# A two-layer graph kernel on one core: layer 0's attention logits laid out with neighbours on partitions

## The chip, the cores and the metric

The kernel runs on one core of a Trainium2 chip. The metric is the device time of one execution in microseconds (us), the median of a few runs of the whole kernel. TensorE (PE) does the matrix products, VectorE (DVE) and ScalarE (ACT) the element-wise work and the reading of PSUM, GpSimd (POOL) some element-wise work on SBUF, and SyncE (SP) issues all DMAs. Each of these runs its own instructions strictly in the order in which the program wrote them.

## The reference, cut to what matters

There are 128 graphs of 64 nodes with 768 features each. Layer 0 is an attention with 12 heads of 64 features, whose logit is a sum of one term of the row node and one term of the neighbour; layer 1 is an ordinary attention with 6 heads.

```python
h = jnp.einsum('bnd,ade->bane', feat_in, W)               # layer 0
th = jnp.tanh(h)
attn = th @ w_src + swapaxes(th @ w_dst, 2, 3)            # [b, a, n, m]: src[n] + dst[m]
attn = jnp.where(attn >= 0, attn, 0.2 * attn)
attn = jnp.where(~adj[:, None], -999.0, attn)
attn = jax.nn.softmax(attn, axis=-1)
feat_out = elu(attn @ h + b)
gate = sigmoid(feat_in @ H_w.T + H_b)
x = layernorm(x + gate * feat_out + (1 - gate) * feat_in)
# layer 1: q, k, v projections, masked softmax attention, output projection,
# residual, layernorm
```

## The kernel before

All arithmetic is float32. The 8192 rows (graph, node) are cut into 64 tiles of 128 rows, so a tile holds two graphs g = 0, 1 of 64 nodes, and two tiles make a pair; there are 32 pairs. Layer 0 runs over the pairs in a software pipeline, then layer 1 runs over groups of four tiles. What passes between the layers (`x1d`, `x1Td`, `vd`) goes through DRAM.

**The order of layer 0.** Each large product (h, the gate g, and layer 1's value v) is a Strassen-like job of seven block products; each of them is three matmuls of 128x384, which the profile shows as six records. The list `TURN` gives the order in which 21 block products are issued in one iteration of the pair loop: h and g of the new pair, v and its rest u of older pairs. Positions 0 to 20 are the places in this list. After each product the earlier one's way out of PSUM is emitted (`flush`, L203), and then the actions that the table `plan` has for this position. So every engine's queue is fixed by this table. In iteration p the new pair's tiles are n0 and n1, and the pair before has t0 and t1; the odd tile goes first.

**What happens to one tile in layer 0.**
- `products` (L354) and `terms` (L363): tanh of h on ACT (L358), two multiplications (L359 on DVE, L360 on POOL), and a reduction (L367) to `sd`, [128, 24]: for each row and head the neighbour ("dst") term and the source ("src") term. The dst terms go to DRAM (`dstd`, L369) and come back broadcast to all 64 rows of their graph (`dd`, [128, 768], two DMAs at L372). SP waits for the first before it issues the second.
- `with_bias` (L380): the bias plus one is added to h on POOL (L383), and half of the heads are copied by two DMAs into `hx` with the graphs exchanged between the partition halves.
- `logits` (L392): one DVE addition makes `att`, rows on partitions, (head, neighbour) along the free dimension. `leaky` (L404) is a Prelu on ACT. `masked` (L408) has three DVE instructions of 768 elements: the predicated copy of -999 (L412), the row maximum (L418), its subtraction (L419). `exps` (L421) is the exponential into `prob`.
- `probs_by_nodes` (L439): six TensorE transposes per tile (helper `transposed`, L432, records at L436), two PSUM banks, two ACT copies (L437) into `pT`, neighbours on partitions.
- `attend` (L450): 24 small matmuls of 64x64 weights by 64x66, in the four quadrants of the array, into two banks `av`; the two extra columns of h are ones and give the softmax's denominator.
- `features`, `elu1`, `gated`, `stats`, `normed`: division (L473, L474), exp (L481), elu (L492), gate and residual (L497, L499), layer norm (L216 to L226). `gate_tanh` (L534) makes the gate on ACT (L537, L538), `residual` (L484) multiplies gate and x on POOL (L487).
- `by_features` (L512): x1 is transposed by six TensorE transposes (`x1Tp`) and two ACT copies for the product v.

`x_sums` (L556) makes the next pair's operand sums on POOL, `value_sums` (L553) those of v on DVE, both through `block_sums` (L143 to L146).

The buffers that matter: the PSUM tag "m" has two banks and is shared by `pTp`, `av` and `x1Tp`; tag "work" has five SBUF buffers of [128, 768].

Of the kernel before, what the change touches and what calls it, by code (L numbers as in the profile page):

```python
# [9 lines left out]
F32 = mybir.dt.float32  # L10
U8 = mybir.dt.uint8
AF = mybir.ActivationFunctionType
ALU = mybir.AluOpType
AX = mybir.AxisListType

P = 128
N = 64
D = 768
KC = D // P
HK = KC // 2  # L20
HALF = D // 2
# [4 lines left out]
J1 = H1 // 2  # L26
LEAKY = 0.2
EPS = 1e-5
NEG0 = -999.0
NEG1 = 9000000000000000.0  # L30
PAIR = 2
GT = 4
# [26 lines left out]
def kernel(  # L59
# [2 lines left out]
    x: bass.AP,  # L62
    xT: bass.AP,
    adj: bass.AP,
    w0: bass.AP,
    b0: bass.AP,
    wsrc: bass.AP,
# [31 lines left out]
    x1_d = [dram.tile([P, PAIR, D], F32, name=f"x1d_{p}") for p in range(NP)]  # L99
    x1T_d = [dram.tile([P, KC, PAIR * P], F32, name=f"x1Td_{p}") for p in range(NP)]  # L100
    v_d = [dram.tile([P, D], F32, name=f"vd_{t}") for t in range(2 * NP)]
    dst_d = [dram.tile([P, H0], F32, name=f"dstd_{t}") for t in range(2 * NP)]


    ident = const.tile([P, P], F32, name="ident")
# [4 lines left out]
    V.memset(minus_one, -1.0)  # L110
    one = const.tile([P, 1], F32, name="one")
    V.memset(one, 1.0)
    neg0 = const.tile([P, 1], F32, name="neg0")
    V.memset(neg0, NEG0)

    def load_cols(src, name):
        t = const.tile([P, KC], F32, name=name)
# [118 lines left out]
    with ExitStack() as ph:  # L236
# [41 lines left out]
        weight_sums(V, wv_w)  # L278

        def work(name):  # L280
            return sb.tile([P, D], F32, tag="work", name=name, bufs=5)

        st = [dict() for _ in range(2 * NP)]

# [78 lines left out]
        def terms(t):  # L363

            th = st[t].pop("th")
            sd = small.tile([P, 2 * H0], F32, tag="sd", name=f"sd_{t}")
            V.tensor_reduce(sd, th.rearrange("p s (a e) -> p (s a) e", e=E0), AX.X, ALU.add)  # L367
            st[t]["sd"] = sd
            nc.sync.dma_start(out=dst_d[t], in_=sd[:, :H0])  # L369
            dd = work(f"dd_{t}")  # L370
            for g in range(2):
                nc.sync.dma_start(  # L372
                    out=dd[g * N : (g + 1) * N, :],
                    in_=dst_d[t][g * N : (g + 1) * N, :]
                    .rearrange("m a -> (m a)")
                    .partition_broadcast(N),
                )
            st[t]["dd"] = dd

        def with_bias(t):  # L380

            h = st[t]["h"]
            G.tensor_tensor(  # L383
                h[:, :, :E0], h[:, :, :E0], b01_bc.unsqueeze(1).to_broadcast([P, H0, E0]), ALU.add
            )

            hx = sb.tile([P, J0, EP], F32, tag="hx", name=f"hx_{t}")
            nc.sync.dma_start(out=hx[:N], in_=h[N:, :J0, :])
            nc.sync.dma_start(out=hx[N:], in_=h[:N, J0:, :])
            st[t]["hx"] = hx  # L390

        def logits(t):  # L392
            sd, dd = st[t].pop("sd"), st[t].pop("dd")
            att = work(f"att_{t}")
            att3 = att.rearrange("p (a m) -> p a m", m=N)
            V.tensor_tensor(
                att3,
                dd.rearrange("p (m a) -> p a m", a=H0),
                sd[:, H0:].unsqueeze(2).to_broadcast([P, H0, N]),
                ALU.add,  # L400
            )
            st[t]["att"] = att

        def leaky(t):  # L404
            att = st[t]["att"]
            S.activation(att, att, AF.Prelu, alpha=LEAKY)

        def masked(t):  # L408

            att = st[t]["att"]  # L410
            att3 = att.rearrange("p (a m) -> p a m", m=N)
            V.copy_predicated(  # L412
                att3,
                st[t]["nadj"].unsqueeze(1).to_broadcast([P, H0, N]),
                neg0.unsqueeze(1).to_broadcast([P, H0, N]),
            )
            mx = small.tile([P, H0], F32, tag="mx", name=f"mx_{t}")
            V.tensor_reduce(mx, att3, AX.X, ALU.max)  # L418
            V.tensor_tensor(att3, att3, mx.unsqueeze(2).to_broadcast([P, H0, N]), ALU.subtract)  # L419

        def exps(t):  # L421

            att = st[t].pop("att")
            prob = work(f"prob_{t}")
            S.activation(
                prob.rearrange("p (j a m) -> p a j m", a=2, m=N),
                att.rearrange("p (a j m) -> p a j m", a=2, m=N),
                AF.Exp,
            )
            st[t]["prob"] = prob  # L430

        def transposed(dst, src, name):  # L432

# [2 lines left out]
                T.transpose(b[:, c * P : (c + 1) * P], src[:, c * P : (c + 1) * P], ident)  # L436
            S.copy(dst, b[:, : 3 * P].rearrange("p (c t) -> p c t", c=3))  # L437

        def probs_by_nodes(t):  # L439
            prob = st[t].pop("prob")  # L440
            pT = sb.tile([P, J0, P], F32, tag="pT", name=f"pT_{t}", bufs=1)
            for half in range(2):
                transposed(
                    pT[:, 3 * half : 3 * half + 3, :],
                    prob[:, half * HALF : (half + 1) * HALF],
                    f"pTp_{t}_{half}",
                )
            st[t]["pT"] = pT

        def attend(t):  # L450
            pT, h, hx = st[t].pop("pT"), st[t].pop("h"), st[t].pop("hx")
            av = [bank("m", f"av_{t}_{a}") for a in range(2)]
            for j in range(J0):
                for a in range(2):
                    rows = slice(a * N, (a + 1) * N)
                    for g in range(2):
                        T.matmul(
                            av[a][g * N : (g + 1) * N, j * EP : (j + 1) * EP],
                            pT[rows, j, g * N : (g + 1) * N],
                            h[rows, a * J0 + j, :] if a == g else hx[rows, j, :],  # L460
                            start=True,
                            stop=True,
                        )
            st[t]["av"] = av
# [60 lines left out]
            nc.sync.dma_start(out=x1T_d[p], in_=x1Ts[p])  # L525

        def mask(p):
            ad = load_adj(sb, 2 * p, PAIR, f"adj_{p}")
            na = sb.tile([P, PAIR, N], U8, tag="nadj", name=f"nadj_{p}", bufs=2)
            V.tensor_scalar(na, ad, 0, None, ALU.is_equal)  # L530
            for i in range(PAIR):
                st[2 * p + i]["nadj"] = na[:, i, :]

        def gate_tanh(t):  # L534

# [27 lines left out]
        for p in range(NP + 2):  # L563
            q = p - 1
            new, old = p < NP, 0 <= q < NP
            t0, t1, n0, n1 = 2 * q, 2 * q + 1, 2 * p, 2 * p + 1
            if new:
                jobs["h"], jobs["g"] = h_job(p), gate_job(p)

            plan = {}  # L570

            def at(pos, ok, *acts):
                if ok:
                    plan.setdefault(pos, []).extend(acts)

            def do(f, *args):
                return lambda: f(*args)

            def v_begins():
                value_sums(q)  # L580
                jobs["v"] = v_job(q)


            at(0, old, do(probs_by_nodes, t1), do(exps, t0), do(gate_tanh, t1))
            at(1, old, do(residual, t1))
            at(2, old, do(attend, t1), do(gate_tanh, t0))
            at(3, old, do(features, t1), do(probs_by_nodes, t0), do(residual, t0))
            at(4, old, do(elu1, t1), do(gated, t1))
            at(5, old, do(attend, t0), do(stats, t1))
            at(6, old, do(features, t0), do(normed, t1))  # L590
            at(7, old, do(elu1, t0), do(gated, t0))
            at(8, old, do(by_features, t1), do(stats, t0))
            at(9, old, do(normed, t0))
            at(12, old, do(v_begins))
            at(15, old, lambda: v_sums[q][0](), lambda: v_sums[q][1](), do(spill_features, q))
            at(16, old, lambda: v_sums[q][2]())
            at(19, old, lambda: v_sums[q][3]())

            at(0, p + 1 < NP, lambda: xTs.__setitem__(p + 1, load_xT(p + 1)))
            at(3, new, do(mask, p))  # L600
            at(4, 0 <= p - 2 < NP, do(spill_values, p - 2))
            at(8, new, do(inputs, p))
            at(11, new, do(products, n1))
            at(11, old, do(by_features, t0))
            at(12, new, do(products, n0))
            at(13, new, do(terms, n1), do(with_bias, n1))
            at(14, new, do(terms, n0), do(with_bias, n0))
            at(15, new, do(plus_one, p))
            at(16, new, do(logits, n1))
            at(17, new, do(leaky, n1))  # L610
            at(17, p + 1 < NP, do(x_sums, p + 1))
            at(18, new, do(masked, n1), do(logits, n0))
            at(19, new, do(exps, n1), do(leaky, n0))
            at(20, new, do(masked, n0))

            for pos, (job, i) in enumerate(TURN):
                ok = {"h": new, "g": new, "v": old, "u": 0 <= p - 2 < NP}[job]
                if ok:
                    step(jobs["u" if job == "u" else job], int(i))
                else:  # L620
                    flush()
                for act in plan.get(pos, ()):
                    act()
            if old:
                jobs["u"] = jobs["v"]
# [290 lines left out]
```

## Time and profile before

| | |
|---|---|
| median of 3 runs | 3061.95 us (3059.85 to 3063.27) |
| the profiled execution | 3063.06 us, of which the span from first to last instruction is 3061.3 us |
| busy in the span | PE 2970.2 us (97%), DVE 1831.3 (60%), ACT 1006.4 (33%), POOL 805.3 (26%) |
| layer 0 | to about 1515 us; one iteration of the pair loop takes 45.6 us |
| one iteration (700 to 746 us) | PE 46.0 of 46.0 us, DVE 38.3, ACT 20.1, POOL 16.5 |
| granted TensorE clock | 0.987 on average, full speed between 100 and 1450 us |

A PE that is shown busy is not proof of a PE at its limit, because matmuls are pipelined and their ends are modelled. The starts of successive groups of matmuls in the timeline are the better measure. The time of the execution is the span and about 1.8 us around it.

### The profile page before, as it was taken

How to read it: one execution, taken by the hardware profiler on the slowest of the kernel's cores; microseconds unless marked ns; L12 is line 12 of the kernel's file. 1: busy time of each engine (PE TensorE's matmuls, PEld its weight loads, DVE VectorE, ACT ScalarE, POOL GpSimd, SP SyncE). 2: the span in 40 equal slices, each digit the busy share in tenths (PEclk: the TensorE clock that was granted, in tenths of full speed). 3: DMA queues.
4: the chain of work that ended last, by engine and by line, in shares of the span. 5: the costliest groups of instructions: out<-in, count | busy, mean ns of one | idle time of the engine just before them, and what ended most of it. 6: DMA issues, size and time to landing. Idle time of an engine off the chain costs nothing. (4 is left out here: it accounts for less than half of the span.)

```text
span 3061.3 us, 42249 instructions
## 1 busy us (share of the span) xinstructions
PE 2970.2 (97%) x16512; PEld 2067.1 (68%) x16512; DVE 1831.3 (60%) x3017; ACT 1006.4 (33%) x1761; POOL 805.3 (26%) x650
## 2 busy tenths in 40 slices
PE   6999999999999999999689999999999999999997
PEld 3666666666666666666378777788777788777784
DVE  5888888888888888888443434343344343344334
ACT  2444444444444444444212222222222222222221
POOL 4333333333333333342112121121212121212111
PEclk8999999999999999999899999999999999999998
DMA  4333333333333333333332211122221222111211
GB/s 166 118 106 115 124 100 115 125 99 115 125 100 117 122 107 117 116 107 111 108 121 69 78 61 56 56 84 83 68 70 45 69 84 78 65 59 51 82 63 62
DMA packets 174917, 284.61 MB, mean 93 GB/s; under 512 B 46208, under 2 KB 112768, under 8 KB 174720
## 3 DMA queue, kind: packets, MB, share of 16 engines
q1 hardware_dynamic: 174720, 281.92, 28.6%
q8 instruction: 131, 2.15, 0.3%
q14 instruction: 66, 0.54, 0.1%
HBM read 167.81 MB, written 101.06 MB: 88 GB/s over the span
## 5 line engine op out<-in xcount | busy, mean ns | idle before, releaser
L487 POOL TENSOR_TENSOR x<-gate,x 128x768 f32<-128x768 f32 x64 | 116.5, 1821 | 331.2 <-ACT gate L538 331.2
L776 POOL TENSOR_TENSOR y<-y,bf_bc 128x768 f32<-128x768 f32 x64 | 114.2, 1815 | 302.7 <-DMA y<-x1d 302.7
L800 DVE TENSOR_TENSOR y<-y_o,y 128x384 f32<-128x384 f32 x128 | 69.8, 554 | 191.1 <-PE y_o L173 183.9
L675 DVE TENSOR_TENSOR kT<-z_k,kT 128x256 f32<-128x256 f32 x96 | 40.6, 423 | 217.3 <-PE z_k L173 109.8
L222 POOL TENSOR_TENSOR rs_b<-ve_b,minus_half 128x1 f32<-128x1 f32 x64 | 35.1, 549 | 498.2 <-DVE ve_b L220 495.3
L173 PE MATMUL y_q<-a,wq 128*128 128x256 f32 x576 | 141.9, 383 | 17.8 <-DMA a<-x1Td 17.8
L143 POOL TENSOR_TENSOR sq_q<-a,a 128x768 f32<-128x768 f32 x16 | 29.5, 1846 | 491.4 <-PE y_o L173 330.5
L360 POOL TENSOR_TENSOR th<-th,wsd 128x768 f32<-128x768 f32 x64 | 115.9, 1812 | 157.8 <-DVE th L359 157.8
L674 ACT ACTIVATE qT<-y_q,bq_c 128x256 f32<-128x256 f32 x144 | 67.3, 468 | 243.6 <-PE y_q L173 221.4
L173 PE MATMUL y_g<-hw,sx_x 128*128 128x384 f32 x384 | 136.2, 492 | 10.5 <-DVE gate L336 10.5
L173 PE MATMUL y_k<-sq_q,wk 128*128 128x256 f32 x576 | 142.8, 385 | 3.7 <-DVE wk L131 3.7
L173 PE MATMUL y_k<-a,wk 128*128 128x256 f32 x576 | 143.5, 385 | 1.8 <-DMA wk<-in_wk_dram 1.8
L173 PE MATMUL y_o<-wf,so_o 128*128 128x384 f32 x384 | 134.8, 495 | 9.0 <-DVE y L800 9.0
L173 PE MATMUL y_h<-w,xT 128*128 128x384 f32 x384 | 136.4, 492 | 7.1 <-DMA w<-in_w_dram 7.1
L173 PE MATMUL z_k<-sq_q,wk 128*128 128x256 f32 x576 | 140.1, 379 | 2.9 <-DVE qT L675 2.9
L173 PE MATMUL z_q<-sq_q,wq 128*128 128x256 f32 x576 | 140.3, 380 | 0.0
L173 PE MATMUL y_q<-sq_q,wq 128*128 128x256 f32 x576 | 140.0, 379 | 0.0
L757 ACT ACTIVATE ctxT<-cp,bv_c 128x256 f32<-128x256 f32 x192 | 75.2, 474 | 197.0 <-PE cp L746 197.0
L173 PE MATMUL z_v<-wv,sv_v 128*128 128x384 f32 x384 | 137.5, 494 | 0.1
L173 PE MATMUL z_h<-w,sx_x 128*128 128x384 f32 x384 | 137.5, 494 | 0.0
L173 PE MATMUL y_v<-wv,x1T 128*128 128x384 f32 x384 | 136.3, 492 | 0.8 <-ACT v L349 0.8
L173 PE MATMUL y_h<-w,sx_x 128*128 128x384 f32 x384 | 135.6, 490 | 1.4 <-DVE w L131 1.4
(163 smaller groups left out, 6756.1 us busy)
## 6 DMA issues: line engine op xcount, KB each, us to landing
xT<-in_xT_dram SPq DMA_DIRECT2D x32, 768.0 KB, 6.9
x<-in_x_dram SPq DMA_DIRECT2D x64, 384.0 KB, 3.6
dd<-dstd SPq DMA_DIRECT2D x128, 192.0 KB, 3.4
x1d<-x SPq DMA_DIRECT2D x64, 384.0 KB, 2.5
x1Td<-x1T SPq DMA_DIRECT2D x32, 768.0 KB, 4.8
vd<-v SPq DMA_DIRECT2D x64, 384.0 KB, 2.9
a<-x1Td SPq DMA_DIRECT2D x64, 384.0 KB, 3.3
v<-vd SPq DMA_DIRECT2D x384, 64.0 KB, 2.3
```

Source lines behind the costliest of these rows:

```text
L143: lambda: eng.tensor_tensor(s1, a21, a22, ALU.add),
L173: T.matmul(to[:, : self.n], lhsT, rhs, start=kc == 0 and not more, stop=kc == HK - 1, skip_group_check=more,)
L222: G.tensor_tensor(rstd, ve, minus_half, ALU.pow)
L360: G.tensor_tensor(th[:, 1, :], th[:, 1, :], wsd[:, 1, :], ALU.mult)
L487: G.tensor_tensor(xp, st[t]["gate"], xp, ALU.mult)
L674: lambda mn, bk_: S.activation(at(*mn), bk_, AF.Identity, bias=bias(mn[1])),
L675: lambda mn, bk_: V.tensor_tensor(at(*mn), bk_, at(*mn), ALU.add),
L757: S.activation(ctxT[g][pr][:, hd, :], cp[a][:, pr * W2 : (pr + 1) * W2], AF.Identity, bias=bv_c[:, hd : hd + 1],)
L776: G.tensor_tensor(y[:, i, :], y[:, i, :], bf_bc, ALU.add)
L800: V.tensor_tensor(at(*mn), b, at(*mn), ALU.add)
```

## The change

The logits of layer 0 are made with the neighbour on the partition. Then the neighbour's term is a per-partition value and the row's source term is what is broadcast: `sd[:, H0:]` goes to DRAM as four rows (head half a, graph g) of 64 x 6 values, and comes back in two DMAs as `ss`, [128, 768]. For the head half a = 1 the graphs are exchanged between the partition halves, so the dst terms of this half are needed exchanged as well; two small DMAs make that copy `dx`. The mask is loaded transposed (`adjT`, arranged on the host) and turned into a `cap` (-300 where there is no edge, 1e30 where there is one), and a minimum replaces the predicated copy. The row maximum and its subtraction are gone. The exponential writes `pT` directly, with a stride of 64 elements, so `probs_by_nodes` with its transposes and copies is gone. `attend` has the same number of matmuls; the quadrants come in another order, and a bank `av[a]` is now written from both row halves of the array. `pT` has two buffers in place of one, "work" four in place of five.

The plan is rearranged: the gate's tanh goes from positions 0 and 2 of the next iteration to 19, the residual from 1 and 3 to 20 and 0, `attend` from 2 and 5 to 1 and 3, and what follows it comes one or two positions earlier; t0's `by_features` goes from 11 to 10; the logits go from 16 and 18 to 17 and 19.

```diff
@@ terms
-            nc.sync.dma_start(out=dst_d[t], in_=sd[:, :H0])
-            dd = work(f"dd_{t}")
-            for g in range(2):
+            nc.sync.dma_start(
+                out=src_d[t].rearrange("(a g) (n j) -> (g n) a j", a=2, j=J0),
+                in_=sd[:, H0:].rearrange("p (a j) -> p a j", j=J0),
+            )
+            ss = work(f"ss_{t}")
+            for r in range(2):
+                rows = src_d[t][0:4:3, :] if r == 0 else src_d[t][1:3, :]
                 nc.sync.dma_start(
-                    out=dd[g * N : (g + 1) * N, :],
-                    in_=dst_d[t][g * N : (g + 1) * N, :]
-                    .rearrange("m a -> (m a)")
-                    .partition_broadcast(N),
+                    out=ss[r * N : (r + 1) * N, :].rearrange("p (a x) -> p a x", a=2),
+                    in_=rows.partition_broadcast(N),
                 )
-            st[t]["dd"] = dd
+            dx = small.tile([P, J0], F32, tag="dx", name=f"dx_{t}")
+            nc.sync.dma_start(out=dx[:N], in_=sd[N:, J0:H0])
+            nc.sync.dma_start(out=dx[N:], in_=sd[:N, J0:H0])
+            st[t]["ss"], st[t]["dx"] = ss, dx
@@ logits, leaky, masked, exps, probs_by_nodes
         def logits(t):
-            sd, dd = st[t].pop("sd"), st[t].pop("dd")
+            sd, ss, dx = st[t].pop("sd"), st[t].pop("ss"), st[t].pop("dx")
             att = work(f"att_{t}")
-            att3 = att.rearrange("p (a m) -> p a m", m=N)
+            for a, d in ((0, sd[:, :J0]), (1, dx)):
+                half = slice(a * HALF, (a + 1) * HALF)
+                V.tensor_tensor(
+                    att[:, half].rearrange("p (n j) -> p n j", j=J0),
+                    ss[:, half].rearrange("p (n j) -> p n j", j=J0),
+                    d.unsqueeze(1).to_broadcast([P, N, J0]),
+                    ALU.add,
+                )
             V.tensor_tensor(
-                att3,
-                dd.rearrange("p (m a) -> p a m", a=H0),
-                sd[:, H0:].unsqueeze(2).to_broadcast([P, H0, N]),
-                ALU.add,
+                att.rearrange("p (x j) -> p x j", j=J0),
+                att.rearrange("p (x j) -> p x j", j=J0),
+                st[t]["cap"].unsqueeze(2).to_broadcast([P, 2 * N, J0]),
+                ALU.min,
             )
...
+        def probs(t):
+            att = st[t].pop("att")
             S.activation(att, att, AF.Prelu, alpha=LEAKY)
...
+            pT = sb.tile([P, 2, J0, N], F32, tag="pT", name=f"pT_{t}")
             S.activation(
-                prob.rearrange("p (j a m) -> p a j m", a=2, m=N),
-                att.rearrange("p (a j m) -> p a j m", a=2, m=N),
+                pT.rearrange("p a j n -> p a n j"),
+                att.rearrange("p (a n j) -> p a n j", a=2, j=J0),
                 AF.Exp,
             )
@@ attend
-                    rows = slice(a * N, (a + 1) * N)
                     for g in range(2):
+                        r = g if a == 0 else 1 - g
+                        rows = slice(r * N, (r + 1) * N)
                         T.matmul(
                             av[a][g * N : (g + 1) * N, j * EP : (j + 1) * EP],
-                            pT[rows, j, g * N : (g + 1) * N],
-                            h[rows, a * J0 + j, :] if a == g else hx[rows, j, :],
+                            pT[rows, a, j, :],
+                            h[rows, j, :] if a == 0 else hx[rows, j, :],
@@ mask
-            ad = load_adj(sb, 2 * p, PAIR, f"adj_{p}")
-            na = sb.tile([P, PAIR, N], U8, tag="nadj", name=f"nadj_{p}", bufs=2)
-            V.tensor_scalar(na, ad, 0, None, ALU.is_equal)
+            ad = sb.tile([P, PAIR, 2 * N], U8, tag="adj", name=f"adj_{p}")
...
+            cap = sb.tile([P, PAIR, 2 * N], F32, tag="cap", name=f"cap_{p}")
+            V.tensor_scalar(cap, ad, BIG, NEG0, ALU.mult, ALU.add)
@@ the plan, after
+            at(0, old, do(probs, t0))
+            at(0, old, do(residual, t0))
+            at(1, old, do(attend, t1))
+            at(2, old, do(features, t1))
+            at(3, old, do(attend, t0), do(elu1, t1), do(gated, t1))
+            at(4, old, do(features, t0), do(stats, t1))
+            at(5, old, do(elu1, t0), do(gated, t0))
+            at(6, old, do(normed, t1), do(stats, t0))
+            at(8, old, do(by_features, t1), do(normed, t0))
+            at(10, old, do(by_features, t0))
...
+            at(17, new, do(logits, n1))
             at(17, p + 1 < NP, do(x_sums, p + 1))
+            at(18, new, do(probs, n1))
+            at(19, new, do(logits, n0), do(gate_tanh, n1), do(gate_tanh, n0))
+            at(20, new, do(residual, n1))
```

More of the change, by code (lines that the diff above doesn't have):

```diff
@@ L28 @@
 EPS = 1e-5
-NEG0 = -999.0
+NEG0 = -300.0
+BIG = 1e30
 NEG1 = 9000000000000000.0
@@ L64 @@
     adj: bass.AP,
+    adjT: bass.AP,
     w0: bass.AP,
@@ L101 @@
     v_d = [dram.tile([P, D], F32, name=f"vd_{t}") for t in range(2 * NP)]
-    dst_d = [dram.tile([P, H0], F32, name=f"dstd_{t}") for t in range(2 * NP)]
+    src_d = [dram.tile([4, N * J0], F32, name=f"srcd_{t}") for t in range(2 * NP)]
     ident = const.tile([P, P], F32, name="ident")
@@ L112 @@
     V.memset(one, 1.0)
-    neg0 = const.tile([P, 1], F32, name="neg0")
-    V.memset(neg0, NEG0)
     def load_cols(src, name):
@@ L280, in work @@
         def work(name):
-            return sb.tile([P, D], F32, tag="work", name=name, bufs=5)
+            return sb.tile([P, D], F32, tag="work", name=name, bufs=4)
         st = [dict() for _ in range(2 * NP)]
@@ L387, in with_bias @@
             hx = sb.tile([P, J0, EP], F32, tag="hx", name=f"hx_{t}")
-            nc.sync.dma_start(out=hx[:N], in_=h[N:, :J0, :])
+            nc.sync.dma_start(out=hx[:N], in_=h[N:, J0:, :])
             nc.sync.dma_start(out=hx[N:], in_=h[:N, J0:, :])
@@ L396, in logits @@
             V.tensor_tensor(
-                att3,
-                dd.rearrange("p (m a) -> p a m", a=H0),
-                sd[:, H0:].unsqueeze(2).to_broadcast([P, H0, N]),
-                ALU.add,
+                att.rearrange("p (x j) -> p x j", j=J0),
+                att.rearrange("p (x j) -> p x j", j=J0),
+                st[t]["cap"].unsqueeze(2).to_broadcast([P, 2 * N, J0]),
+                ALU.min,
             )
             st[t]["att"] = att
-        def leaky(t):
-            att = st[t]["att"]
+        def probs(t):
+            att = st[t].pop("att")
@@ L406, in leaky @@
             S.activation(att, att, AF.Prelu, alpha=LEAKY)
[L408 to L419, printed above, removed]
@@ L421, in exps @@
-        def exps(t):
-            att = st[t].pop("att")
-            prob = work(f"prob_{t}")
+            pT = sb.tile([P, 2, J0, N], F32, tag="pT", name=f"pT_{t}")
             S.activation(
-                prob.rearrange("p (j a m) -> p a j m", a=2, m=N),
-                att.rearrange("p (a j m) -> p a j m", a=2, m=N),
+                pT.rearrange("p a j n -> p a n j"),
+                att.rearrange("p (a n j) -> p a n j", a=2, j=J0),
                 AF.Exp,
             )
-            st[t]["prob"] = prob
+            st[t]["pT"] = pT
@@ L437, in transposed @@
             S.copy(dst, b[:, : 3 * P].rearrange("p (c t) -> p c t", c=3))
[L439 to L448, printed above, removed]
         def attend(t):
@@ L527, in mask @@
         def mask(p):
-            ad = load_adj(sb, 2 * p, PAIR, f"adj_{p}")
-            na = sb.tile([P, PAIR, N], U8, tag="nadj", name=f"nadj_{p}", bufs=2)
-            V.tensor_scalar(na, ad, 0, None, ALU.is_equal)
+            ad = sb.tile([P, PAIR, 2 * N], U8, tag="adj", name=f"adj_{p}")
+            nc.sync.dma_start(
+                out=ad, in_=adjT[PAIR * p : PAIR * (p + 1)].rearrange("t p a n -> p t (a n)")
+            )
+            cap = sb.tile([P, PAIR, 2 * N], F32, tag="cap", name=f"cap_{p}")
+            V.tensor_scalar(cap, ad, BIG, NEG0, ALU.mult, ALU.add)
             for i in range(PAIR):
-                st[2 * p + i]["nadj"] = na[:, i, :]
+                st[2 * p + i]["cap"] = cap[:, i, :]
         def gate_tanh(t):
@@ L581, in v_begins @@
                 jobs["v"] = v_job(q)
[L584 to L593, printed above, removed]
+            at(0, old, do(probs, t0))
[8 more added lines that the diff above has]
+            at(10, old, do(by_features, t0))
             at(12, old, do(v_begins))
@@ L603 @@
             at(11, new, do(products, n1))
-            at(11, old, do(by_features, t0))
             at(12, new, do(products, n0))
@@ L608 @@
             at(15, new, do(plus_one, p))
-            at(16, new, do(logits, n1))
-            at(17, new, do(leaky, n1))
+            at(17, new, do(logits, n1))
             at(17, p + 1 < NP, do(x_sums, p + 1))
-            at(18, new, do(masked, n1), do(logits, n0))
-            at(19, new, do(exps, n1), do(leaky, n0))
-            at(20, new, do(masked, n0))
+            at(18, new, do(probs, n1))
+            at(19, new, do(logits, n0), do(gate_tanh, n1), do(gate_tanh, n0))
+            at(20, new, do(residual, n1))
             for pos, (job, i) in enumerate(TURN):
@@ L888 @@
         "adj": g["adj"].reshape(B * N, N),
+        "adjT": np.stack(
+            [
+                g["adj"].reshape(B // 2, 2, N, N)[:, order].transpose(0, 1, 3, 2).reshape(B // 2, P, N)
+                for order in ([0, 1], [1, 0])
+            ],
+            axis=2,
+        ),
         "w0": g["L0_gnn_W"].transpose(1, 0, 2).reshape(D, D),
```

## The prediction

> **What bounds the kernel now.** I read the page's shares first, then the waits of PE between 100 and 1450 us (there it waits for nothing), then the timelines of one iteration of layer 0.
>
> ```profile
> PE 2970.2 (97%) x16512; PEld 2067.1 (68%) x16512; DVE 1831.3 (60%) x3017; ACT 1006.4 (33%) x1761; POOL 805.3 (26%) x650
> ```
> ```profile
> 699.80 2.10 PE L173 MATMUL y_h<-w,xT 128*128 128x384 f32 x6
> 701.74 0.82 PE L436 MATMUL pTp<-ident,prob 128*128 128x128 f32 x6
> 702.39 2.10 PE L173 MATMUL x_h<-w,xT 128*128 128x384 f32 x6
> ...
> 709.26 0.95 PE L436 MATMUL pTp<-ident,prob 128*128 128x128 f32 x6
> 710.05 2.10 PE L173 MATMUL y_h<-w,sx_x 128*128 128x384 f32 x6
> ...
> 720.79 0.82 PE L436 MATMUL x1Tp<-ident,x 128*128 128x128 f32 x6
> ...
> 745.39 2.10 PE L173 MATMUL y_h<-w,xT 128*128 128x384 f32 x6
> ```
>
> Columns: start, duration, what. Each group starts where its predecessor lets it: a block product every 1.935 us, and the whole iteration is 745.39 - 699.80 = 45.59 us. Products (21 x 1.935 = 40.64), two `attend` blocks (0.86 each and 0.2 around each), x1's transposes (2 x 0.65) and those of `prob` (702.39 - 701.74 = 0.65 and 710.05 - 709.26 = 0.79) add up to it. So layer 0 is **bound by PE**, and only what leaves PE's queue shortens it, as long as the others keep up. DVE is nearest (38.3 us in 700 to 746). The second thing to see is who locks whom:
>
> ```profile
> 737.10 1.20 POOL L144 TENSOR_TENSOR sx_x<-sx_x,xT 128x384 f32<-128x384 f32 x1
> 738.25 1.31 POOL L145 TENSOR_TENSOR sx_x<-xT 128x384 f32<-128x384 f32 x1
> ```
> ```profile
> 737.36 0.55 DVE L350 TENSOR_TENSOR v<-x_v,v 128x384 f32<-128x384 f32 x1
> 737.82 0.89 DVE L145 TENSOR_TENSOR sv_v<-x1T 128x384 f32<-128x384 f32 x1
> 738.63 2.24 DVE L396 TENSOR_TENSOR att<-dd,sd 128x768 f32<-128x768 f32 x1
> ```
>
> DVE L145 ends 0.4 us after POOL L144, L396 ends 1.3 us after POOL L145, though alone they take 0.55 and 1.52; L350, with one input in PSUM, is not held up. Between two DVE instructions without dependence, POOL gets in. The third is SP's chain:
>
> ```profile
> 732.26 0.33 SPq L369 DMA_DIRECT2D dstd<-sd  x1
> 734.05 1.11 SPq L372 DMA_DIRECT2D dd<-dstd  x2
> 735.26 0.54 SPq L388 DMA_DIRECT2D hx<-h  x1
> 735.85 0.59 SPq L389 DMA_DIRECT2D hx<-h  x1
> 736.53 0.54 SPq L369 DMA_DIRECT2D dstd<-sd  x1
> 738.96 1.10 SPq L372 DMA_DIRECT2D dd<-dstd  x2
> ```
>
> SP stands for 1.8 and 2.4 us until `dstd` has landed; `dd` lands 3.4 us after its own issue.
>
> **What the Trainium skill says.** "SBUF — State Buffer", section Who interferes with whom: a DVE instruction with two SBUF inputs and a GpSimd instruction that reads SBUF exclude each other for a whole instruction. The trace agrees (lines above). The same page, SBUF cachelines: accesses that step to another 16-byte line pay; L396, which reads `dd` at 48 bytes, takes 1.52 us where L419 takes 0.96; ACT's strided write is not in this trace. "TensorEngine Tiling (Array Packing)", Gotcha 1: different row tiles write to different PSUM banks and cannot use one at the same time. In the trace each `av` bank has one row half, so nothing shows what both do.
>
> **The change part by part**, per iteration, for a steady one.
>
> *PE.* 12 transposes go: 0.65 + 0.79 = **1.44 us**. `attend` keeps 48 matmuls; I take 0.86 us per block as before. If the new bank assignment pairs the row halves off, its 0.72 us of matmuls would double, at most +1.44; a gain has no source, all four quadrants already overlap. PE alone: 45.59 - 1.44 = 44.15 us.
>
> *DVE.* Per tile L396 (1.86 mean), L412 (1.085), L418 (0.953) and L419 (0.958) go, 4.86 us. Two additions of 384 (0.47 from start to start, as L145 of DVE alone) and a minimum of 768 (0.96, as L419) come: 1.9. The mask L530 took 1.70 only because residuals (L487) ran beside it; alone it took 0.22, for the cap's 256 elements I take 0.35. DVE falls by 2 x 3 + 1.3 = 7 us and cannot be the bound by its sum. *ACT* loses four copies (L437, 0.48). Its exponential keeps 0.84 if the write stride of 256 bytes is free; at L396's ratio 1.52/0.96 it takes 1.3 to 1.6. I take 0.84. These are hidden by PE unless they lie on the chain below.
>
> *The moved steps make a new chain*, and here the question is decided. I set zero at the first transposes of x1 of t1 (720.79 before); times below are my sums of durations above.
> - t0's transposes now stand one product earlier, so ACT copies them (0.86) ahead of h's last copy: `sd` of n1 is ready at 12.5 (11.4 before: 732.23 - 720.79).
> - SP: source terms written 12.5, `ss` issued 14.3 and 14.9, then two `dx` (0.6 each, new), two `hx`, and the second tile's write at 18.0. Before, that write stood behind `hx` and `dd` in the queues and took 2.4; with `ss` landed by 18.4 I take 1.7 to 2.4. Pieces of 24 bytes, 256 in place of 128: 0.1 more (the 768 4-byte pieces of each bias column load land under 0.5 us apart). Then `ss` of n0 goes out at 20.1 and 20.7, and lands 3.4 later: **24.2**, up to 24.8; its `dx` is there at about the same time.
> - n1's logits start when POOL's third sum ends (19.85; `ss` landed before) and end at 21.75. Prelu, exp, tanh and add, 0.84 to 0.86 each, free the gate at 25.07, and POOL's residual of n1 (1.81) starts at **25.15**, n0's behind it.
> - n0's logits: additions at 24.2 and 24.7, minimum 25.2 to 26.1, or, where POOL has just taken the port, 27.0 to 28.0. Then Prelu and exp (1.7), the copy of h's first product (0.5), its addition (0.5) and `features` (1.5), since they stand in line behind on ACT and DVE: done at 32.1 at worst. PE comes to t0's `attend`, which needs these two "m" banks, at 33.5.
> - From there exp, elu1, gated, cap, v, features of t0, stats, elu1 and gated of t0, sh_a and ACT's L226 take 12.0 one after another to x1 of t1: 44.1, where PE comes at 44.15.
>
> So the chain just fits, with almost no slack. Iteration 44.15 against 45.59, 30 times: -43. At the start the first attend no longer waits for transposes and copies, some -2. In the last iteration, with only v left, PE waits for this chain anyhow (x1's second transposes stood at 1498.07, 47.65 after the last zero; now at about 42.6): -5. Sum -50, against the profiled 3063.06: 3013; the median lies 1.1 lower, 3012. I add 2 for small waits: **3014**. Layer 1 and the SBUF loads before are not touched.
>
> **The rivals.**
> 1. *The port takes the gain back, slower.* If n0's `ss` lands after 24.7, its second addition loses the port to the residual of n1, the minimum to that of n0 (DVE and POOL alternate, as above): 25.15 + 1.8 + 0.47 + 1.8 + 0.47 + 0.96 = 30.6 in place of 28.0. `features` ends at 34.7, x1 at 46.7; an iteration takes 46.7, +1.1 x 30 = +34, less the ends' -5: about 3092. For it: 0.5 us decides, and POOL's two residuals are placed exactly there. Against: `ss` took its full landing of 3.4 in my sum, and the write has less before it. With a slow exponential (+0.6) the threshold moves out too, but each iteration pays for one or two of them: 3030 to 3110.
> 2. *Partial gain.* The landing is as worked out, but exp or the minimum costs 0.2 to 1 us on the chain: iterations of 44.4 to 45.2, 3020 to 3050. The same view speaks for it: slack below 0.1.
> 3. *The banks pair off the row halves*: +1.4 per iteration, gain gone, 3055 to 3062: no change. For it only the skill's sentence.
>
> **How the numbers follow.** PE bound as worked out, 3008 to 3020: 0.42. Partial gain: 0.20. No change, by rival 3 or by a share of rival 1: 0.08. Slower: 0.30. A difference under about 0.2% (6 us) can't be told from none. Faster 0.62, same 0.08, slower 0.30. The likeliest case alone reaches from 3008 to 3022; the range 3008 to 3092 leaves out a slow exponential together with the lost port, and a PE that gains more than its transposes.
>
> **What would show it.** Right: starts of y_h at position 0 are 44.15 us apart, no PE waits between 100 and 1450, L414 (minimum) at most 1.9 us long. Wrong: PE waits at `av` for `fo` L465 and at `x1Tp` for ACT L229, L408 or L414 over 2 us in n0 while L478 runs, the exponential L426 above 1 us, or an `attend` block of 1.5 us.

## The result, and the profile after

The changed kernel takes 3073.94 us (median of 4 runs, 3070.20 to 3077.63) where the kernel before takes 3062.61 (4 runs, 3059.85 to 3063.66) beside it. The ratio is 1.0038, with a 95% interval of 1.0021 to 1.0056: **slower by 0.4%**, where 3014 was forecast. The profiled execution took 3070.20 us, of which the span is 3068.4; the granted clock is 0.987 as before.

The page's first part, of the kernel after:

```profile
PE 2935.1 (96%) x16128; PEld 2028.0 (66%) x16128; DVE 1696.5 (55%) x2952; ACT 998.3 (33%) x1633; POOL 844.3 (28%) x650
```

The work went as the change says: PE has 384 records fewer and 35.1 us less to do, DVE 134.8 us less. So the time was not lost to more work but to standing still. The timeline of PE, after, from one position 0 to the next but one:

```profile
704.13 2.10 PE L176 MATMUL y_h<-w,xT 128*128 128x384 f32 x6
...
726.32 0.87 PE L437 MATMUL x1Tp<-ident,x 128*128 128x128 f32 x6 [0.31 <-ACT x L229]
...
741.23 2.10 PE L176 MATMUL y_g<-hw,xT 128*128 128x384 f32 x6
744.25 2.17 PE L176 MATMUL y_v<-wv,sv_v 128*128 128x384 f32 x6 [0.92 <-DVE sv_v L147]
...
752.06 2.10 PE L176 MATMUL y_h<-w,xT 128*128 128x384 f32 x6
...
797.47 2.10 PE L176 MATMUL y_h<-w,xT 128*128 128x384 f32 x6
```

The first of these iterations takes 752.06 - 704.13 = 47.93 us, the next 797.47 - 752.06 = 45.41. Taken so over layer 0, there are **two kinds of iteration**: after the first two intervals, in which the pipeline fills, 20 of 29 take 45.2 to 45.7 us (mean 45.4) and nine take 47.4 to 48.0 (mean 47.7; called struck below). Before, all take 45.6; forecast were 44.15. The waits of PE between 100 and 1450 us, after (columns: who waited for what, us in total, times, longest); before, this view is empty:

```profile
PE y_v L176 <- DVE sv_v L147: 26.8, 29, 0.9
PE y_h L176 <- ACT h L323: 5.3, 9, 0.6
PE av L448 <- DVE rden L464: 3.7, 7, 0.6
PE x1Tp L437 <- ACT x L229: 3.6, 12, 0.3
PE av L448 <- issue: 2.8, 9, 0.3
```

The first wait is in every iteration. The others come only in some, and they are what is left of a longer delay on another engine. Both kinds can be followed on DVE.

**The wait in every iteration.** L147 is the second sum of `value_sums`, an operand of PE's product at position 17. DVE's timeline, after:

```profile
737.17 1.74 DVE L370 TENSOR_REDUCE sd<-th 128x24 f32<-128x1536 f32 x1
...
739.88 1.75 DVE L370 TENSOR_REDUCE sd<-th 128x24 f32<-128x1536 f32 x1
741.54 1.29 DVE L146 TENSOR_TENSOR sv_v<-x1T 128x384 f32<-128x384 f32 x1
742.87 1.23 DVE L147 TENSOR_TENSOR sv_v<-sv_v,x1T 128x384 f32<-128x384 f32 x1
```

L147 ends at 744.10, and PE starts at 744.25. Its neighbour had started at 741.23, so 3.02 us lie between the two starts in place of 1.935: the product is 1.09 late. (The view shows 0.92, as it counts from the neighbour's modelled end, 743.33.) Nothing on DVE stands idle there. The reduction of n0 ahead of the two sums ends at 741.63, 15.3 us after t1's x1 transposes (726.32), and then L146 and L147 each last 1.2 to 1.3 us, where such a sum takes 0.55 alone: POOL's `with_bias` and first sum (739.09 to 743.69) lock the port. The lock is not new: in the kernel before, the same two sums take 1.29 and 1.24 us. What is new is that they start later.

**The wait in nine iterations.** DVE's logits of n0, after, first in the long and then in the short of the two iterations above:

```profile
705.00 1.47 DVE L408 TENSOR_TENSOR att<-ss,sd 128x384 f32<-128x384 f32 x1 [3.00 <-DMA ss<-srcd]
706.39 2.16 DVE L408 TENSOR_TENSOR att<-ss,dx 128x384 f32<-128x384 f32 x1
708.58 0.96 DVE L414 TENSOR_TENSOR att<-att,cap 128x768 f32<-128x768 f32 x1
...
751.38 0.56 DVE L408 TENSOR_TENSOR att<-ss,sd 128x384 f32<-128x384 f32 x1 [1.46 <-DMA ss<-srcd]
751.86 0.55 DVE L408 TENSOR_TENSOR att<-ss,dx 128x384 f32<-128x384 f32 x1
752.45 2.46 DVE L414 TENSOR_TENSOR att<-att,cap 128x768 f32<-128x768 f32 x1
```

```profile
704.24 3.90 POOL L478 TENSOR_TENSOR x<-gate,x 128x768 f32<-128x768 f32 x2 [2.66 <-ACT gate L533]
...
752.18 4.41 POOL L478 TENSOR_TENSOR x<-gate,x 128x768 f32<-128x768 f32 x2 [2.67 <-ACT gate L533]
```

The two POOL lines are its residuals (two in each record). In the short iteration both additions have begun before the residuals come at 752.18, and only the minimum L414 is locked out once. In the long one `ss` has landed 1.5 us later, the residuals are already there, and DVE is locked out twice, as it and POOL alternate. The minimum ends at 709.54, 5.4 us after PE's position 0 (704.13); in the short one it ends at 754.91, 2.9 after (752.06). The same holds through layer 0: POOL's residuals start 0.10 to 0.12 us after PE's position 0 in all 29 iterations, and in the nine long ones, and only there, n0's second addition starts after them. In five of the nine both additions are locked out, in four the second addition and the minimum.

### The profile page after: what moved, and what is told of

Read it like the earlier page. It is cut to its first block, busy times and chain, and to the rows that moved or that the text cites. A ratio compares the mean times of both kernels' runs of the same rounds, so it can differ in the third digit from the quotient of the medians.

```text
span 3068.4 us, 41354 instructions
## 1 busy us (share of the span) xinstructions
PE 2935.1 (96%) x16128; PEld 2028.0 (66%) x16128; DVE 1696.5 (55%) x2952; ACT 998.3 (33%) x1633; POOL 844.3 (28%) x650
## 5 line engine op out<-in xcount | busy, mean ns | idle before, releaser
L225 POOL TENSOR_TENSOR rs_a<-ve_a,minus_half 128x1 f32<-128x1 f32 x64 | 55.9, 873 | 473.2 <-DVE ve_a L223 473.2
L225 POOL TENSOR_TENSOR rs_b<-ve_b,minus_half 128x1 f32<-128x1 f32 x64 | 35.1, 549 | 497.8 <-DVE ve_b L223 494.8
L146 POOL TENSOR_TENSOR sq_q<-a,a 128x768 f32<-128x768 f32 x16 | 29.5, 1846 | 490.2 <-PE y_o L176 327.7
L176 PE MATMUL y_v<-wv,sv_v 128*128 128x384 f32 x384 | 136.7, 492 | 27.9 <-DVE sv_v L147 27.9
L478 POOL TENSOR_TENSOR x<-gate,x 128x768 f32<-128x768 f32 x64 | 135.8, 2142 | 94.6 <-ACT gate L533 83.0
L362 DVE TENSOR_TENSOR th<-th,wsd 128x768 f32<-128x768 f32 x64 | 73.1, 1142 | 151.5 <-ACT th L361 151.5
```

The lines of the kernel that those rows point to most:

```text
L146: lambda: eng.tensor_tensor(s1, a21, a22, ALU.add),
L176: T.matmul(to[:, : self.n], lhsT, rhs, start=kc == 0 and not more, stop=kc == HK - 1, skip_group_check=more,)
L225: G.tensor_tensor(rstd, ve, minus_half, ALU.pow)
L362: V.tensor_tensor(th[:, 0, :], th[:, 1, :], wsd[:, 0, :], ALU.mult)
L478: G.tensor_tensor(xp, st[t]["gate"], xp, ALU.mult)
```

## The experiments

Each kernel has 4 runs, and its ratio is to the kernel before on the same chip. e1 to e4 ran beside a kernel before of 3063.88 us, e5 to e7 of 3061.70, e8 and e9 of 3062.44. "Iterations" are the 29 after the first two intervals.

**e1, the move of t0's `by_features` undone, and nothing else** (is the late L147 the cost of this move?):

```diff
-            at(10, old, do(by_features, t0))
+            at(11, old, do(by_features, t0))
```

> The changed kernel with one plan entry undone: t0's by_features back at position 11 (it went to 10 in the change). Theory A (the gain is eaten by three things: PE's 0.92 us wait per iteration for the v sum of DVE L147, the port lock between n0's logits and POOL's residuals in about 9 of 30 iterations, and the slower exponential): sd of n1 is ready 1.07 us earlier, the wait of y_v for L147 goes (26.8 us to under 3), whole kernel about 30 us faster than the changed one, 3038 to 3050; some iterations of over 46.5 us remain. Theory B (the DMA round trip of the source terms is what holds everything): the whole chain is earlier by 1.07 us, but L147 does not hang on a DMA, so the time moves by less than 10 us.

Measured: 3049.08 us (3045.61 to 3056.17), ratio 0.9957 (0.9941 to 0.9973). The wait for L147 is gone from PE's waits: 14 iterations now take 44.1 to 44.6 us. But 15 take 46.3 to 46.9: the late landing still strikes. That these are 15 and not nine says little, as the profiled execution is the longest of e1's four (3056.17) and that of the change the shortest (3070.20). At about 2.3 us for each struck iteration, the medians stand for some 12 and 11 (an estimate). So the move from 11 to 10 is the cause of the wait in every iteration, and there is a second loss beside it.

**e2, the residual L478 on DVE** (are POOL's residuals the second loss?):

```diff
-            G.tensor_tensor(xp, st[t]["gate"], xp, ALU.mult)
+            V.tensor_tensor(xp, st[t]["gate"], xp, ALU.mult)
```

> The changed kernel with the residual's product (L478) on DVE in place of POOL, at the same places of the plan. Theory A: without POOL's two instructions of 1.8 us the additions and the minimum of n0 take 0.55, 0.55 and 0.96 us in every iteration; the 9 iterations of 47.3 to 48 us become 45.2 to 46; the wait for L147 stays at 0.92; whole kernel 15 to 25 us faster than the changed one, 3050 to 3060. Theory B: DVE waits for the landing of ss as before (up to 3.0 us), the long iterations stay above 47, change under 6 us.

Measured: 3044.06 us (3043.71 to 3048.30), ratio 0.9941 (0.9926 to 0.9956). All iterations but one take 45.2 us. The waits of PE between 100 and 1450 us, in e2, are two lines:

```profile
PE y_v L176 <- DVE sv_v L147: 26.9, 29, 0.9
PE x1Tp L437 <- ACT x L229: 0.3, 1, 0.3
```

The long iterations are gone and the wait for L147 stands unchanged, so the two losses are separate. DVE has one instruction more per tile and the kernel is 30 us faster than the change.

**e3, exponential with unit stride, `attend` reading its weights with a step instead** (does the exponential's stride cost?):

```diff
-            pT = sb.tile([P, 2, J0, N], F32, tag="pT", name=f"pT_{t}")
+            pT = sb.tile([P, 2, N, J0], F32, tag="pT", name=f"pT_{t}")
-                pT.rearrange("p a j n -> p a n j"),
+                pT,
-                            pT[rows, a, j, :],
+                            pT[rows, a, :, j],
```

> The changed kernel with pT in the order (head half, node, head): the exponential writes contiguous elements, and attend reads its 64 weights with a step of 24 bytes. Theory A: the exponential L426 takes 0.84 us in place of 1.56; the chain is up to 1.4 us shorter in the long iterations and 0.3 in the others, but POOL's residuals come 0.7 us earlier and meet n0's additions more often: 0 to 15 us faster, 3059 to 3074. If weights with a step cost PE time, the attend block grows from 0.96 us between its neighbours' starts to more, at most 1.7, and the kernel gets up to 40 us slower. Theory B: under 6 us either way as long as attend keeps its time.

Measured: 3089.92 us (3088.84 to 3092.16), ratio 1.0088 (1.0071 to 1.0105); iterations of 46.6 to 46.8 us. The exponential, by the tile `pT` (lowest, median and highest ns), in the change and then in e3:

```profile
L426 ACT ACTIVATE pT<-att x64: 1502/1558/1576, 58.0 to 1493.0; 128x768 f32<-128x768 f32 x64
```
```profile
L426 ACT ACTIVATE pT<-att x64: 842/843/847, 58.2 to 1512.7; 128x768 f32<-128x768 f32 x64
```

The stride thus costs 0.72 us per tile. But the step moves to the weights. Groups between 100 and 1450 us (count, busy us, mean ns), in the change and then in e3:

```profile
L448 PE MATMUL av<-hx,pT 64*64 64x66 f32 x1416 | 54.3, 222 | 2.8 <-issue 2.8
L448 PEld LDWEIGHTS av<-hx,pT 64*64 64x64 f32 x1416 | 46.4, 134 | 3.8 <-issue 3.8
```
```profile
L448 PE MATMUL av<-hx,pT 64*64 64x66 f32 x1392 | 92.9, 279 | 0.0
L448 PEld LDWEIGHTS av<-hx,pT 64*64 64x64 f32 x1392 | 84.8, 204 | 0.0
```

A weight load takes 204 ns where it took 134 in the change. From the start of the product before an `attend` block to that of the product after it, e3 takes 719.74 - 716.18 = 3.56 us and the change 708.96 - 706.07 = 2.89. Twice 0.67 more is 1.34 per iteration, and 45.24 (an iteration with the wait for L147 alone, as in e2) + 1.34 = 46.58 is about what is measured. So e3 answers what a strided weight read costs, but says little on the exponential, since PE's own work was longer. e5 was made for that.

**e4, e1 and e2 together:**

> Both edits together: t0's by_features at position 11 and the residual on DVE. Theory A: PE has nothing left to wait for in most iterations, which come to 44.2 to 44.5 us; whole kernel 3012 to 3025, faster than the kernel before by 38 to 50 us. Theory B: the source terms' round trip keeps iterations above 45: 3040 or more.

Measured: **3012.50 us** (3011.92 to 3013.51), ratio 0.9835 (0.9820 to 0.9850), the fastest kernel of the study. Every iteration takes 44.13 to 44.22 us, and PE waits for nothing between 100 and 1380 us. Its timeline shows that the product that waited 0.92 us in the change (the second line) now follows its neighbour after 1.93 us:

```profile
714.94 2.10 PE L176 MATMUL y_g<-hw,xT 128*128 128x384 f32 x6
716.87 2.17 PE L176 MATMUL y_v<-wv,sv_v 128*128 128x384 f32 x6
718.88 2.10 PE L176 MATMUL z_g<-hw,sx_x 128*128 128x384 f32 x6
```

On DVE the reduction of n0 ends at 714.25, now 14.2 us after t1's transposes (700.02) and not 15.3, and L147 at 716.73. PE starts 0.14 after that, as closely as in the change, where it stood waiting (744.10 and 744.25): the product is just not late any more.

**e5, exponential written contiguously into `pT`, the rest as in the change**:

```diff
-                pT.rearrange("p a j n -> p a n j"),
-                att.rearrange("p (a n j) -> p a n j", a=2, j=J0),
+                pT.rearrange("p a j n -> p (a j n)"),
+                att,
```

> The changed kernel with the exponential writing its 768 values one after another into pT, so that the probabilities stand there in the order (node, head) while attend reads them as (head, node): what is left out is that reordering, and layer 0's attention is not the reference's; the amount of work is the same. Theory A (strided writing costs 0.7 us per exponential and twice that on the chain, the port lock remains): L426 takes 0.84 us, the long iterations shrink from 47.3-48 to about 46-46.5, the others stay at 45.2 to 45.4 because PE's 0.92 us wait for L147 holds them: 3052 to 3066. Theory B (the exponential is off the path, only the source terms' landing counts): within 4 us of the changed kernel, long iterations still above 47.

Measured: 3084.82 us (3083.83 to 3087.80), ratio 1.0078 (1.0063 to 1.0093). The exponential takes 0.84 us, all else is as in the change, and the kernel is **11 us slower than the change** (the intervals of the two ratios do not overlap). Groups of DVE between 100 and 1450 us, in the change and then in e5:

```profile
L408 DVE TENSOR_TENSOR att<-ss,dx 128x384 f32<-128x384 f32 x60 | 47.4, 791 | 0.1
L414 DVE TENSOR_TENSOR att<-att,cap 128x768 f32<-128x768 f32 x60 | 87.8, 1463 | 2.1
```
```profile
L408 DVE TENSOR_TENSOR att<-ss,dx 128x384 f32<-128x384 f32 x59 | 76.0, 1288 | 0.0
L414 DVE TENSOR_TENSOR att<-att,cap 128x768 f32<-128x768 f32 x59 | 74.3, 1260 | 2.0
```

The second addition has become longer, the minimum shorter: the lock-out has moved ahead. The gate comes after n1's exponential in ACT's queue, so a shorter exponential frees the residuals earlier: in e5's timelines they start 0.52 us before PE's position 0 (710.41 against 710.93), in the change 0.11 after (704.24 against 704.13). There they find n0's additions still to come (the second starts at 712.56 and takes 2.15 us) in nearly every iteration: all but two take 46.1 to 46.7 us.

**e6, the source terms written as one run of 48 bytes per partition instead of two of 24** (the same number of bytes):

```diff
-                out=src_d[t].rearrange("(a g) (n j) -> (g n) a j", a=2, j=J0),
-                in_=sd[:, H0:].rearrange("p (a j) -> p a j", j=J0),
+                out=src_d[t].rearrange("q (m x) -> (q m) x", x=H0),
+                in_=sd[:, H0:],
```

> The changed kernel with the source terms written to DRAM as one run of 48 bytes per partition in place of two of 24, so that they stand there in the order (row, head) and come back in a wrong order: what is left out is their arrangement, the logits are not the reference's; bytes and instructions are the same. If the small pieces make the round trip long and uneven, SP's wait from this write to ss falls from 1.6-2.6 (first tile) and 1.75-3.3 us (second) to the 1.4-1.8 and 2.1-2.9 that the kernel before shows or below, fewer iterations lose the port, and the time falls by 5 to 20 us to 3054-3069. If the spread comes from what else is in the DMA queues, the waits keep their spread and the time stays within 5 us.

Measured: 3046.05 us (3043.61 to 3053.29), ratio 0.9953 (0.9939 to 0.9968). All iterations but one take 45.2 to 45.3 us; in that one (47.39) it is the read of `ss` that lands late, 5.1 us after its issue. One of the four executions took 3053.29 us; what lengthened it is not traced. The waits of DVE between 100 and 1450 us, the line for `ss`, in the change and then in e6:

```profile
DVE att L408 <- DMA ss<-srcd: 47.5, 30, 3.0
```
```profile
DVE att L408 <- DMA ss<-srcd: 20.8, 30, 1.9
```

On SP, from the issue of the write to that of `ss` (SP stands there until the write has landed), the change shows 1.57 to 2.61 us for a pair's first tile and 1.74 to 3.26 for its second; in e6 it is 1.41 to 1.91 and 1.65 to 2.05. So the small pieces are what made the landing late, and the late landing is what made the long iterations, as POOL's residuals stay on POOL here. e6 changes both the number of pieces and their size, and doesn't tell which of them counts.

**e7, the kernel before with its residual on DVE** (is e2's gain just that DVE is a better place?); the edit is e2's.

> The kernel before with its residual's product (L487) on DVE in place of POOL. Theory A: before, no wait of PE hung on POOL's port, and DVE had 7 us of room per iteration, so the time stays within 4 us of 3063 (iterations of 45.5 to 45.7 us); the move is worth something only together with the changed plan. Theory B (DVE's room is used up by the moved work): more than 6 us slower.

Measured: 3077.29 us (3073.77 to 3079.46), ratio 1.0048 (1.0031 to 1.0064), and iterations of 46.1 us: slower, which I had not expected. The waits of PE between 100 and 1450 us, and DVE's timeline, both of e7:

```profile
PE pTp L436 <- DVE fo L474: 5.1, 29, 0.2
```
```profile
715.57 0.96 DVE L487 TENSOR_TENSOR x<-gate,x 128x768 f32<-128x768 f32 x1 [2.10 <-ACT gate L538]
```

The residual holds DVE's queue for the gate 2.1 us long, and `features` L474, which empties the "m" bank for the next transposes, stands behind it. The view shows 0.2 us of it, but the whole cost lies at these transposes: from the start of the product before them to that of the product after them, e7 takes 718.89 - 715.57 = 3.32 us, and the kernel before 710.05 - 707.22 = 2.83, which is the 0.49 by which an iteration is longer. It shows that e2 gains nothing by the engine as such: the same edit costs 15 us before and gains 30 after.

**e8, e1 and e6 together:**

> The changed kernel with two edits: t0's by_features at position 11, and the source terms written as one run of 48 bytes per partition (their arrangement is left out, so the logits are not the reference's; bytes and instructions are the same). The residuals stay on POOL. Theory A (the loss is PE's 0.92 us wait for L147 plus the late landing of the 24-byte pieces, which loses the port to POOL): both causes are gone, nearly all iterations come to 44.15 us, 3010 to 3025. Theory B (POOL's residuals cost time whatever the landing): 16 of 30 iterations stay above 46 as they do with the first edit alone, 3040 or more.

Measured: 3013.68 us (3010.88 to 3014.01), ratio 0.9837 (0.9823 to 0.9852); iterations of 44.13 to 44.56 us. Two unlike cures of the second loss, taking POOL off the port (e4) and landing in time (e8), end at one value, that of a PE without waits.

**e9, e5 and e2 together:**

> The changed kernel with the exponential writing one element after another (its reordering is left out, so layer 0's attention is not the reference's) and the residual's product on DVE. Theory A (the short exponential was slower only because POOL's residuals then met n0's additions more often): without POOL there it does no harm, all iterations at 45.24 us, within 4 us of the kernel that has the residual on DVE alone, 3040 to 3048. Theory B (something else in the contiguous write or in the other order of the probabilities slows the kernel): iterations of 46 to 46.7 us stay, 3070 or more.

Measured: 3045.13 us (3043.66 to 3046.61), ratio 0.9942 (0.9925 to 0.9958), iterations of 45.2 us, as e2 with its long exponential. Where POOL isn't on the port, 0.72 us more or less of exponential is worth nothing: it acts only through the moment at which the residuals start. e4 says the same at the faster pace: there it takes 1.56 us, and yet x1 of t1 is ready at 743.22 and PE takes it at 744.22, with 1.0 us to spare.

## Why the prediction was wrong, point by point

**PE's own work: right.** 45.59 - 1.44 = 44.15 was the sum, and e4 measures 44.15. `attend` takes 0.86 us from its first matmul to the next product as before, though each `av` bank is written from both row halves. Rival 3 is refuted; the sentence of the Trainium skill it rested on ("TensorEngine Tiling (Array Packing)", Gotcha 1) does not hold for the two halves of a bank used here. The likeliest case, 3012 by the sum and 3014 with small waits, is what e4 and e8 take, in which the two losses are gone.

**The failed step: "a new chain", followed to one of its two ends.** That `sd` is ready 1.1 us later, since t0's transposes come one product earlier, was in the first item of the chain. From there I followed only SP. On DVE, L146 and L147 stand behind the same reductions, and PE waits for L147 at position 17. The part on DVE said "cannot be the bound by its sum" and asked for no deadline. The trace of before already shows the same two sums, locked by POOL, and PE's product behind them:

```profile
734.87 1.29 DVE L143 TENSOR_TENSOR sv_v<-x1T 128x384 f32<-128x384 f32 x1
736.20 1.24 DVE L144 TENSOR_TENSOR sv_v<-sv_v,x1T 128x384 f32<-128x384 f32 x1
...
737.58 2.17 PE L173 MATMUL y_v<-wv,sv_v 128*128 128x384 f32 x6
```

L144 ends at 737.44 and PE starts 0.14 later (0.14 to 0.16 in every iteration between 100 and 1400 us). In the change PE waits for this sum, and starts 0.15 after it too. So before there was no time to spare that the trace shows, and a delay of 1.1 us had to reach PE almost whole. Carried on in the prediction's own terms: n1's `sd` at 12.5 as I had it, n0's 2.7 later, and two sums of 1.3 and 1.2 end at 17.7, where PE comes at 16.8 (737.58 - 720.79 before). Cost: 45.24 (e2) - 44.15 (e4) = 1.09 us per iteration, the delay found above from start to start; over the 30 steady iterations some 33 us. e1 and e4 show it.

**The mis-sized term: the write of the source terms.** "Pieces of 24 bytes, 256 in place of 128: 0.1 more", taken from 4-byte pieces of bias loads, gave 1.8 us for the first write and 1.7 to 2.4 for the second. They take up to 2.61 and 3.26. (Those loads were also issued about 0.5 us apart, so their spacing could not show what their pieces cost.) With "up to 24.8" for the landing and 24.7 as rival 1's threshold there was nothing to spare, and nine iterations fall on the wrong side. In these `ss` of n0 lands 1.0 us later than in the other twenty, on average against PE's position 0; the two writes ahead of it take 0.4 and 0.5 of that, the read under 0.1. e6 shows it by experiment.

**Rival 1's mechanism: right, its extent not.** I had put the threshold as a switch for all iterations: 46.7 where lost, +2.55 over 44.15. A struck iteration costs 47.7 - 45.4 = 2.3, and e1's struck ones (46.3 to 46.9) lie where rival 1 put them. But the landing scatters, so only nine are struck: 9 x 2.3 = 21 us. "DVE and POOL alternate", read from two pairs of lines before, held in every struck iteration; that an instruction holds the port for its whole length is what the Trainium skill says ("SBUF — State Buffer", Who interferes with whom), and the 2.16 us of L408 beside a residual agree. That the kernel came out slower, which rival 1 alone had forecast, is in good part chance: its own loss of 21 us would have left a gain of some 29, and the larger part is the wait for L147, which no rival had.

**The exponential: mis-sized, harmless alone.** Taken at 0.84, bounded by 1.3 to 1.6, measured at 1.56. That accesses which step to another line pay is what the Trainium skill says ("SBUF — State Buffer", SBUF cachelines), and the trace agrees (1.56 against 0.84). I had also written that a slow exponential moves rival 1's threshold out, but that each iteration pays for it. The first is right: e5, which takes the slowness away, is slower. The second is wrong: e9 and e2 agree to about a microsecond (3045.13 and 3044.06), and e4 and e8 reach 44.15 with the long exponential. The chain was summed with a fast exponential and a minimum locked out once, and came to 44.1; without the lock, the slow exponential had room.

**The sum.** The steps of x1 of t1 in layer 0's last iteration came to 1508.72 us, where they stood at 1498.07: +10.65, while -50 was forecast. Of these 61 us, 33 are L147, 21 the struck iterations, 3 the start (-1.1 in place of -2) and the end (-3.1 in place of -5), and the remaining 4 are small waits of unstruck iterations (45.4 in place of 45.24) and rounding. e4's -51 between the medians closes it from the other side.

## What to carry to other kernels

When a step is moved, follow every reader of what it delays to the engine that waits last, and set each end against that engine's arrival: here the delay was written down, for one of two readers. A start that follows its operand as closely in the old trace as it does where it is known to wait has no time to spare that can be counted on. A step with 0.1 us to spare behind a DMA round trip must be read as a share of iterations that miss, from the scatter of that landing and not from its typical value. And where two engines exclude each other, the moment at which an instruction starts can matter more than its length: a shorter exponential cost 11 us, and moving the residual off POOL gained 30 in one order of work and lost 15 in another.

## What the runs showed of the hardware

- ACT's exponential of 128x768 takes 0.84 us with contiguous output and 1.56 with a step of 256 bytes, at the same input.
- Weights read with a step of 24 bytes: a load 204 ns against 134, a 64x66 matmul 279 against 222, and 48 of them in four quadrants put 1.63 us between the products around them against 0.96.
- The same 6 KB written to DRAM in 256 pieces of 24 bytes hold SP 1.57 to 3.26 us until they have landed, and in 128 pieces of 48 bytes 1.41 to 2.05. Both are below the 512 bytes that the Trainium skill names as the least for full rate ("DMA: Bandwidth & Descriptors", Specifications), so that figure doesn't part them; here the piece decided whether the landing could be relied on.
- DVE and POOL took turns at the port they share: beside POOL's two residuals (3.90 us for both) the two additions on DVE took 1.47 and 2.16 us in place of 0.55, each ending after the residual ahead of it; so in all nine long iterations.
